# Softplus of a selective scan moved into the matmul's PSUM bank, its bias into ScalarE's operations, with a new order of the side jobs

## The chip, the core and the metric

The kernel runs on one core of a Trainium2 chip. The metric is the device time of one execution in microseconds (us), the median over several runs. A profile of one further execution is at hand. The core has five engines that each work through a queue of their own in order: TensorE (PE in the profile, its weight loads PEld), VectorE (DVE), ScalarE (ACT), GpSimd (POOL) and SyncE (SP, which only issues DMAs here). ScalarE issues DMAs too. Engines wait for one another through semaphores. SBUF is the working memory; PSUM is the memory that TensorE writes its results to, in banks of 512 float32 values for each of the 128 partitions.

## What is computed

The program is a two-layer decoder on 16 blocks of 128 tokens, 512 wide. Five stages follow one another: a state space scan (SSM), a cross attention, a ternary feed-forward network, attention of the second layer, and a mixture of experts. The change lies in the first stage only. In the reference that is:

```python
A = -jnp.exp(A_log)                                   # (512, 16)
dt = jax.nn.softplus(jnp.einsum('bld,ed->ble', x, dt_proj_w) + dt_proj_b)
bc = jnp.einsum('bld,ed->ble', x, x_proj_w) + x_proj_b
Bs, Cs = (bc[..., :d_state], bc[..., d_state:])       # d_state = 16

def step(h, inputs):
    xt, dtt, Bt, Ct = inputs
    dA = jnp.exp(dtt[..., None] * A)
    dBx = (dtt * xt)[..., None] * Bt[:, None, :]
    h = dA * h + dBx
    y = jnp.einsum('bdn,bn->bd', h, Ct)
    return (h, y)
...
return jnp.einsum('bld,md->blm', y, out_proj_w) + out_proj_b
```

Both kernels write softplus(z) as max(z, 0) + ln(1 + exp(-|z|)), with a correction for the rounding of 1 + e: with v = exp(-|z|) and u = 1 + v as rounded, dt = ln(u) + (max(z, 0) - ((u - 1) - v)).

## The kernel before

**Tiling.** The features stand on the partitions (four chunks of 128, `KC`), the tokens on the free axis. Two blocks of tokens make one state (`st` in the code; `BQ` = 2, `TQ` = 256 tokens), so there are eight states. For each state the loop runs over the 16 state dimensions n of the SSM; a pair (state, n) is a unit u, and the loop at lines 371 to 438 goes over all 128 units. I call the position n within a state a step of the loop.

**One unit.** ScalarE makes the decays of unit u+1 (`decays`, line 301: one small copy and four Exp over 254 columns, into the PSUM tile h, two buffers). GpSimd makes dBx of unit u+2 (`terms`, 316; three buffers). VectorE scans unit u (`scan`, 323). For most units VectorE also multiplies by C (tile hC); for the units that `shared` (321) picks, GpSimd does that (tile hs, two buffers). TensorE adds the result into the sums py by transposing (`add`, 338), one unit later, or two for shared ones. B and C of a unit come by a DMA that spreads one row over the partitions (`widths_in`, 311, four units ahead, tile BC, six buffers).

**Side jobs between the units.** At fixed steps n the loop also does, for the next state (`nxt`): `widths` (x_proj) and `widths_out`; the product for the step sizes in two halves h of two chunks each (`step_product`, 194, with the bias as a further small bf16 matmul of a three-row split of dtb against ones); the softplus in `step_exp`, `step_one`, `step_rest`, `step_log`, `step_sum` (204 to 229). The tiles are pd (PSUM), sp_v and sp_u (SBUF), then dt and dtx. For the state behind (`back`): `sums_out`, `turn_back`, `turned_out`, `output` and `output_sum`. And 64 products of keys and values for later stages (`keys_values`, 269), each evacuated by ScalarE (`keys_values_out`, 287) in the following unit and stored by a DMA that ScalarE issues; the last one of a block of tokens also has the next block loaded (`fetch`).

**Order and banks.** In the loop each instruction is pinned to program order on its engine (`pinned`, 71); ahead of the loop the planner of the framework orders them. The side jobs share two PSUM banks, A and B, one buffer each (`bank`, 126). The dictionary `at` (424) says at which steps a key/value product is made and in which bank.

**Ahead of the loop** (lines 130 to 367): the weights are loaded, both bias rows are split into three bf16 rows by GpSimd, then widths, the step sizes of the first state by halves, two loads of ctx, one key/value product, the first decays and the first two dBx.

## Time and profile before

| | us |
|---|---|
| median of three runs (3026.57 to 3032.8) | 3029.26 |
| the profiled execution, its own time | 3033.7 |
| its span, first to last instruction | 3031.8 |
| start of the first scan | 29.66 |
| start of the scan of the last unit | 502.65 |
| mean granted TensorE clock | 0.992 |

Busy time over the whole span: TensorE 2927.2 us (97%), VectorE 1920.5, GpSimd 1490.4, ScalarE 1356.5. The profile gives the line of a helper as L66: it is the line in `Pinned` through which all pinned instructions go, so in the loop instructions are told apart by their tiles. A timeline row reads: start, duration, engine, line, operation, output<-inputs, partitions x elements, count, and in brackets how long the engine had been idle and who released it. The slices of the span are 75.8 us each:

```profile
## 2 busy tenths in 40 slices
PE   8999999999999999999999999999999999999998
PEld 6666665455555555555787556666566666666665
DVE  6989998766776676665887897567643322242224
ACT  5776775333343343345344797655433322222221
POOL 8999996534334334332333663356435553333331
```

### The profile page before, as it was taken

Reading aid. Unit: us, or ns where it says so; the run is one execution under the profiler, and the core shown is the slowest. Engines: PE = TensorE matmul, PEld = TensorE weight load, DVE = VectorE, ACT = ScalarE, POOL = GpSimd, SP = SyncE. Lnnn points to the kernel's source line nnn. Section 1 sums busy time; section 2 is a strip of 40 time slices with the busy share of each in tenths; the row PEclk is TensorE's granted clock in tenths of the full one; section 3 lists DMA queues with packets and bytes.
Section 4 is the critical chain, followed back from the end, with each engine's and each line's share of the span. In section 5 each row is a group of like instructions: output and inputs, shape, how many; then the busy total and the mean of one; then the engine's idle time right before and its main releaser. Section 6 shows DMA issues by size and latency. Waiting matters only on the chain.

```text
span 3031.8 us, 40699 instructions
## 1 busy us (share of the span) xinstructions
PE 2927.2 (97%) x13744; PEld 1830.9 (60%) x13744; DVE 1920.5 (63%) x4221; ACT 1356.5 (45%) x3315; POOL 1490.4 (49%) x1274
## 2 busy tenths in 40 slices
PE   8999999999999999999999999999999999999998
PEld 6666665455555555555787556666566666666665
DVE  6989998766776676665887897567643322242224
ACT  5776775333343343345344797655433322222221
POOL 8999996534334334332333663356435553333331
PEclk9999999999999999999999999999999999999999
DMA  6654444880000000024000200234357665555541
GB/s 199 205 138 126 121 126 135 266 285 14 8 11 11 8 11 11 8 66 143 1 1 1 70 1 8 64 115 164 136 174 241 221 226 164 165 192 165 164 150 61
DMA packets 171603, 331.58 MB, mean 109 GB/s; under 512 B 22078, under 2 KB 80958, under 8 KB 169852
## 3 DMA queue, kind: packets, MB, share of 16 engines
q1 hardware_dynamic: 126988, 219.91, 23.9%
q0 software_dynamic: 19200, 64.16, 6.3%
q10 hardware_dynamic: 25200, 44.84, 3.9%
q8 instruction: 111, 1.82, 0.2%
q14 instruction: 104, 0.85, 0.1%
HBM read 244.57 MB, written 137.43 MB: 126 GB/s over the span
## 4 chain that ended last, share of the span: by engine, by line
PE 67%; DVE 13%; ACT 3%; POOL 1%; issue 1%; DMA 1%; SPq 0%; another core or an unknown queue 0%; DVEq 0%; ACTq 0%; POOLq 0%
PE y L1830 8%; PE pu L1813 7%; PE pg L1813 7%; PE pq L676 7%; PE po L796 6%; PE po L1008 4%; PE ao L785 3%; PE sc L745 3%; PE pt L536 2%; PE pg L988 2%; PE pu L988 2%; PE pT L773 1%; PE ptx L536 1%; PE pkv L66 1%; PE pw L1482 1%
## 5 line engine op out<-in xcount | busy, mean ns | idle before, releaser
L765 POOL TENSOR_TENSOR pr<-pr,sm 128x512 f32<-128x512 f32 x128 | 135.4, 1058 | 369.2 <-DVE sm L764 273.8
L66 POOL TENSOR_TENSOR dBx<-dtx,BC 128x1024 f32<-128x1024 f32 x126 | 298.6, 2394 | 1.0 <-DMA BC<-bcd 0.4
L1813 PE MATMUL pg<-gu,xgT 128*128 128x352 f32 x784 | 297.1, 461 | 1.4 <-ACT act L1816 1.4
L1813 PE MATMUL pu<-gu,xgT 128*128 128x352 f32 x784 | 296.9, 460 | 0.0
L758 ACT ACTIVATE pr<-sc,mx,sf 128x256 f32<-128x256 f32 x256 | 142.2, 560 | 332.8 <-DVE mx L751 304.7
L1817 DVE SCALAR_TENSOR_TENSOR act<-pu,row,act 128x352 f32<-128x352 f32 x98 | 57.1, 582 | 358.4 <-PE pu L1813 339.2
L1830 PE MATMUL y<-dn,aT 128*128 128x512 f32 x588 | 268.3, 592 | 0.0
L1858 POOL TENSOR_TENSOR x<-got,x 128x512 f32<-128x512 f32 x120 | 151.7, 1270 | 225.8 <-DMA got<-results,gidx 224.6
L66 ACT ACTIVATE h<-dt,negA 128x254 f32<-128x254 f32 x508 | 242.2, 477 | 16.9
L796 PE MATMUL po<-w,aT 128*128 128x512 f32 x512 | 233.1, 593 | 1.9 <-DVE aT L790 1.9
L676 PE MATMUL pq<-w,xT 128*128 128x512 f32 x512 | 230.8, 593 | 0.6 <-DVE m L642 0.6
L1851 POOL DMA_INDIRECT got<-results,gidx x120 | 116.2, 969 | 227.6 <-DMA results<-yo 200.5
L66 DVE TENSOR_TENSOR_SCAN h<-h,dBx 128x1024 f32<-128x1024 f32 x80 | 183.2, 2290 | 34.3 <-ACT h L66 24.9
L1813 PEld LDWEIGHTS pu<-gu,xgT 128*128 128x128 f32 x784 | 149.3, 191 | 83.0 <-issue 0.5
L1816 ACT ACTIVATE act<-pg 128x352 f32<-128x352 f32 x98 | 45.5, 464 | 304.5 <-PE pg L1813 265.3
L1813 PEld LDWEIGHTS pg<-gu,xgT 128*128 128x128 f32 x784 | 141.6, 191 | 65.1 <-ACT act L1816 1.9
L647 POOL TENSOR_TENSOR m<-m,m 128x512 f32<-128x512 f32 x96 | 122.5, 1276 | 111.3 <-DVE m L642 108.0
L66 PE MATMUL pkv<-w,cT 128*128 128x512 f32 x384 | 171.6, 593 | 1.4 <-ACT y L66 1.1
L1842 DVE COPY yo<-y 128x512 f32<-128x512 f32 x90 | 62.2, 691 | 165.4 <-PE y L1830 157.9
L1830 PEld LDWEIGHTS y<-dn,aT 128*128 128x128 f32 x588 | 104.1, 190 | 100.8 <-issue 94.2
L1805 ACT COPY xgT<-ptx 128x512 f32<-128x512 f32 x98 | 57.4, 586 | 235.9 <-PE ptx L536 221.4
L998 POOL TENSOR_TENSOR lo<-sg,hi 128x512 fp32r<-128x512 f32 x64 | 84.2, 1316 | 155.4 <-ACT hi L997 155.3
(413 smaller groups left out, 6792.0 us busy)
## 6 DMA issues: line engine op xcount, KB each, us to landing
bucket<-zeros SPq DMA_DIRECT2D x96, 388.0 KB
row<-bucket SPq DMA_DIRECT2D x90, 388.0 KB
BC<-bcd SPq DMA_DIRECT2D x128, 256.0 KB
results<-yo ACTq DMA_DIRECT2D x90, 256.0 KB
gu<-in_moe_guT SPq DMA_DIRECT2D x16, 1408.0 KB
x_k<-kv ACTq DMA_DIRECT2D x32, 256.0 KB
x_v<-kv ACTq DMA_DIRECT2D x32, 256.0 KB
v<-x_v SPq DMA_DIRECT2D x32, 256.0 KB
```

The lines of the kernel that those rows point to most:

```text
L66: return self.tc.keep_in_program_order(call(*args, **kw))
L647: nc.gpsimd.tensor_tensor(m1, m1, m2, ALU.add)
L676: nc.tensor.matmul(ps, src[:, c], w[c], start=c == 0, stop=c == KC - 1)
L758: nc.scalar.activation(pr[:, j], st.sc[g, i][:, j], AF.Exp, scale=st.sf[:, h : h + 1], bias=st.mx[g, i][:, j : j + 1], accum_out=sm[:, j : ...
L765: nc.gpsimd.tensor_tensor(pr, pr, sm.unsqueeze(2).to_broadcast([P, 2, 2 * P]), ALU.mult)
L796: nc.tensor.matmul(st.po, aT[:, j], k.wo[h // 8][:, h % 8], start=h == 0, stop=h == G * J - 1)
L988: nc.tensor.matmul(p[:, e], w[:, c, at : at + P], sn.qT[:, :, c], start=c == 0, stop=c == KC - 1)
L1008: nc.tensor.matmul(sn.po[i], part[:, e, i * P : (i + 1) * P], k.fd[hc // 8][:, hc % 8], start=hc == 0 and part is parts[0], stop=hc == 15 ...
L1813: nc.tensor.matmul(ps, u.xT[:, c], gu[:, c, lo : lo + I], start=c == 0, stop=c == KC - 1)
L1830: self.nc.tensor.matmul(u.y, u.aT[:, c], u.w[1][:, c], start=c == 0, stop=c == 2)
L1851: nc.gpsimd.indirect_dma_start(out=got[:, :], out_offset=None, in_=k.results[h][g][0:end, :], in_offset=bass.IndirectOffsetOnAxis(ap=self. ...
L1858: nc.gpsimd.tensor_tensor(k.x[b], got, k.x[b], ALU.add)
```

## The change

- **Bias.** The step sizes' bias is no longer added by matmuls. It is loaded as a column per chunk (dtb, 128 x 4) and given to ScalarE as the bias of Relu and Abs. Of the two split rows only that of the output projection is left.
- **Softplus in the bank.** Max(z, 0) goes to the SBUF tile sp_m and |z| to sp_u, by ScalarE, chunk by chunk. Exp(-|z|) is written back to pd in PSUM; the correction, the sum and the step size are then computed in pd by VectorE. `step_sum` moves from GpSimd to VectorE; dtx is made by it from pd and x; a new `step_out` has ScalarE copy dt out of the bank.
- **Who multiplies by C.** `shared` now picks seven of 16 units (n = 4, 6, 7, 8, 12, 13, 14) instead of three of eight (1, 4, 6).
- **Positions in a state.** Logs at 6 and 12, rest at 6 and 12, sums at 7 and 13, copies out at 8 and 14; outputs at 5 and 8 and their sums at 6 and 9; the key/value products at new steps and banks.
- **Ahead of the loop.** The order is pinned. The key/value weights and the first ctx loads are issued earlier. The first state's step sizes are computed by quarters (`first_steps`), quarters 0 and 1 in bank A, 2 and 3 in bank B, with max(z + b, 0) made by VectorE. Two key/value products are made in the banks of py.

```diff
-        rows = [cst.tile([65, D], BF16, name=f"rows_{n}") for n in ("dtb", "outb")]
+        dtb = cst.tile([P, KC], F32, name="dtb")
+        row = cst.tile([65, D], BF16, name="row_outb")
...
-        load_row(0)
+        keep(nc.sync.dma_start(dtb, a["dtb"].rearrange("(c p) -> p c", p=P)))
...
-            nc.scalar.dma_start(dtw[:, :, es], a["dtwT"][:, es].rearrange("(c p) e -> p c e", p=P))
...
+            keep(nc.scalar.dma_start(dtw[:, :, es], a["dtwT"][:, es].rearrange("(c p) e -> p c e", p=P)))
+        kvw = k.wslot().rearrange("p (s c e) -> p s c e", s=2, c=KC)
+        for i, n in enumerate(("wk", "wv")):
+            keep(nc.scalar.dma_start(kvw[:, i], a["x2_" + n + "T"].rearrange("(c p) e -> p c e", p=P)))
...
         negA = cst.tile([P, KC, NS], F32, name="negA")
         nc.scalar.activation(negA, alog, AF.Exp)
...
-                    q.nc.tensor.matmul(st.pd[h][:, e], dtw[:, c, at : at + P], st.xT[:, c], start=c == 0, stop=False)
-                q.nc.tensor.matmul(st.pd[h][:, e], rows[0][:, at : at + P], ones, start=False, stop=True)
+                    q.nc.tensor.matmul(st.pd[h][:, e], dtw[:, c, at : at + P], st.xT[:, c], start=c == 0, stop=c == KC - 1)
...
+        def step_exp(st, h):
+            m = wk.tile([P, 2, TQ], F32, tag="sp_m", name="sp_m", bufs=1)
+            u = wk.tile([P, 2, TQ], F32, tag="sp_u", name="sp_u", bufs=1)
+            st.mu[h] = m, u
+            for to, what in ((m, AF.Relu), (u, AF.Abs)):
+                for e in range(2):
+                    q.nc.scalar.activation(to[:, e], st.pd[h][:, e], what, bias=dtb[:, 2 * h + e : 2 * h + e + 1])
+            q.nc.scalar.activation(st.pd[h], u, AF.Exp, scale=-1.0)
 
         def step_one(st, h):
-            v, u = st.vu[h]
-            q.nc.scalar.activation(u, v, AF.Identity, bias=1.0)
+            q.nc.scalar.activation(st.mu[h][1], st.pd[h], AF.Identity, bias=1.0)
+
+        def step_log(st, h):
+            q.nc.scalar.activation(st.dt[:, 2 * h : 2 * h + 2], st.mu[h][1], AF.Ln)
 
         def step_rest(st, h):
-            v, u = st.vu[h]
-            q.nc.vector.scalar_tensor_tensor(v, u, 1.0, v, ALU.subtract, ALU.subtract)
-            q.nc.vector.scalar_tensor_tensor(v, st.pd[h], 0.0, v, ALU.max, ALU.subtract)
+            m, u = st.mu[h]
+            q.nc.vector.scalar_tensor_tensor(st.pd[h], u, 1.0, st.pd[h], ALU.subtract, ALU.subtract)
+            q.nc.vector.tensor_tensor(st.pd[h], m, st.pd[h], ALU.subtract)
 
         def step_sum(st, h):
             hs = slice(2 * h, 2 * h + 2)
-            q.nc.gpsimd.tensor_tensor(st.dt[:, hs], st.dt[:, hs], st.vu[h][0], ALU.add)
-            q.nc.gpsimd.tensor_tensor(st.dtx[:, hs], st.dt[:, hs], st.xT[:, hs], ALU.mult)
+            q.nc.vector.tensor_tensor(st.pd[h], st.dt[:, hs], st.pd[h], ALU.add)
+            q.nc.vector.tensor_tensor(st.dtx[:, hs], st.pd[h], st.xT[:, hs], ALU.mult)
+
+        def step_out(st, h):
+            q.nc.scalar.copy(st.dt[:, 2 * h : 2 * h + 2], st.pd[h])
+
+        def first_steps(st, c, room):
+            h, e = divmod(c, 2)
+            if e == 0:
+                st.pd[h] = bank("AB"[h], [P, 2, TQ], "pd")
+            pd, (m, u) = st.pd[h][:, e], [r[:, c] for r in room]
+            at = c * P
+            for i in range(KC):
+                q.nc.tensor.matmul(pd, dtw[:, i, at : at + P], st.xT[:, i], start=i == 0, stop=i == KC - 1)
+            q.nc.vector.tensor_scalar(m, pd, dtb[:, c : c + 1], 0.0, ALU.add, ALU.max)
+            q.nc.scalar.activation(u, pd, AF.Abs, bias=dtb[:, c : c + 1])
+            q.nc.scalar.activation(pd, u, AF.Exp, scale=-1.0)
+            q.nc.scalar.activation(u, pd, AF.Identity, bias=1.0)
+            q.nc.scalar.activation(st.dt[:, c], u, AF.Ln)
+            q.nc.vector.scalar_tensor_tensor(pd, u, 1.0, pd, ALU.subtract, ALU.subtract)
+            q.nc.vector.tensor_tensor(pd, m, pd, ALU.subtract)
+            q.nc.vector.tensor_tensor(st.dt[:, c], st.dt[:, c], pd, ALU.add)
+            q.nc.gpsimd.tensor_tensor(st.dtx[:, c], st.dt[:, c], st.xT[:, c], ALU.mult)
...
-        shared = lambda u: u % 8 in (1, 4, 6)
+        shared = lambda u: u % 16 in (4, 6, 7, 8, 12, 13, 14)
...
         first = states[0]
+        q.nc = pinned(tc)
+        for _ in range(2):
+            fetch()
         widths(first, xT0)
         widths_out(first)
...
         for u in range(4):
             widths_in(u)
+        room = [wk.tile([P, KC, TQ], F32, tag="hC", name="room", bufs=3) for _ in range(2)]
+        for c in range(KC):
+            first_steps(first, c, room)
         decays(0)
         terms(0)
         terms(1)
+        keys_values(None, ps_y.tile([P, D], F32, tag="py0", name="pkv"))
+        keys_values_out()
+        keys_values(None, ps_y.tile([P, D], F32, tag="py1", name="pkv"))
+        q.nc.scalar.dma_start(outw, a["outwT"].rearrange("(c p) e -> p c e", p=P))
...
             if nxt:
                 if n == 3:
                     widths_out(nxt)
+                if n in (8, 14):
+                    step_out(nxt, n // 14)
                 if n in (5, 9):
                     step_exp(nxt, n // 9)
                 if n in (6, 10):
                     step_one(nxt, n // 10)
+                if n in (6, 12):
+                    step_log(nxt, n // 12)
...
-            if n in (4, 8) and back:
-                output_sum(back, n // 8)
-            if n in (7, 11) and nxt:
-                step_rest(nxt, n // 11)
-            if n in (8, 13) and nxt:
+            if n in (6, 9) and back:
+                output_sum(back, n // 9)
+            if n in (6, 12) and nxt:
+                step_rest(nxt, n // 12)
+            if n in (7, 13) and nxt:
                 step_sum(nxt, n // 13)
...
-                if n in (3, 7):
-                    output(back, n // 7)
+                if n in (5, 8):
+                    output(back, n // 8)
...
-            at = {5: "B", 9: "B", 11: "B", 12: "A", 13: "B", 14: "A", 15: "B"}
+            at = {2: "B", 6: "B", 9: "B", 11: "B", 12: "B", 14: "B", 15: "A"}
             if not back:
-                at |= {0: "A", 1: "B", 3: "B", 7: "B"}
+                at |= {0: "B", 3: "B", 7: "B"}
             if not nxt:
-                at |= {2: "A", 4: "A", 8: "A"}
+                at |= {3: "A", 4: "A", 7: "A"}
...
-            if n in (7, 11) and nxt:
-                step_log(nxt, n // 11)
```

## The prediction

> **What bounds the kernel now.** I read the 40 slices first: the change touches the first stage only, which fills slices 1 to 7, and there TensorE, VectorE and GpSimd all stand at 6 to 9 tenths. Then I cut that stage into the eight states (two blocks of 128 tokens, 16 scan steps each), from each state's second scan to the next's:
>
> ```profile
> core 0: us, PE busy (x) PEld busy (x) DVE busy (x) ACT busy (x) POOL busy (x), PEclk, DMA share, GB/s
> 33.13:94.20 61.07, 59.59 (x364) 47.18 (x365) 54.02 (x31) 43.78 (x100) 55.01 (x27) 0.97 0.73 200
> ...
> 271.71:332.27 60.56, 56.80 (x282) 37.41 (x280) 55.34 (x33) 43.57 (x101) 56.61 (x27) 1.00 0.45 130
> ...
> 453.38:502.65 49.27, 47.94 (x246) 31.51 (x244) 42.37 (x25) 34.80 (x81) 45.61 (x20) 1.00 0.40 122
> ```
>
> A middle state takes 60.56 us (the six of them 359.2 in sum, two being 59.30 and 57.64) while three engines have 55 to 57 us of work. No engine is full, so the time is in waits; VectorE's scan never stops for long, so I read its timeline over one state:
>
> ```profile
> 211.14 2.29 DVE L66 TENSOR_TENSOR_SCAN hs<-h,dBx 128x1024 f32<-128x1024 f32 x1 [1.02 <-POOL dBx L66]
> 215.09 2.30 DVE L66 TENSOR_TENSOR_SCAN h<-h,dBx 128x1024 f32<-128x1024 f32 x1 [1.66 <-ACT h L66]
> ...
> 224.34 0.67 DVE L66 TENSOR_TENSOR x<-po,x 128x512 f32<-128x512 f32 x1
> ...
> 235.24 4.21 DVE L66 SCALAR_TENSOR_TENSOR sp_v<-sp_u,sp_v 128x512 f32<-128x512 f32 x1
> 239.55 0.69 DVE L66 SCALAR_TENSOR_TENSOR sp_v<-pd,sp_v 128x512 f32<-128x512 f32 x1
> 240.16 2.29 DVE L66 TENSOR_TENSOR_SCAN h<-h,dBx 128x1024 f32<-128x1024 f32 x1
> ...
> 253.38 0.83 DVE L66 SCALAR_TENSOR_TENSOR sp_v<-sp_u,sp_v 128x512 f32<-128x512 f32 x1
> 254.32 0.69 DVE L66 SCALAR_TENSOR_TENSOR sp_v<-pd,sp_v 128x512 f32<-128x512 f32 x1
> 254.93 2.28 DVE L66 TENSOR_TENSOR_SCAN hs<-h,dBx 128x1024 f32<-128x1024 f32 x1
> ...
> 267.08 2.30 DVE L66 TENSOR_TENSOR_SCAN h<-h,dBx 128x1024 f32<-128x1024 f32 x1 [0.42 <-POOL dBx L66]
> ```
>
> The same operation, both inputs in SBUF, takes 0.83 us once and 4.21 once. GpSimd's timeline says why:
>
> ```profile
> 234.23 4.66 POOL L66 TENSOR_TENSOR dBx<-dtx,BC 128x1024 f32<-128x1024 f32 x2
> 240.38 1.26 POOL L66 TENSOR_TENSOR dt<-dt,sp_v 128x512 f32<-128x512 f32 x1 [1.49 <-DVE sp_v L66]
> ```
>
> VectorE's operation ends 0.56 us after GpSimd's two products (238.89) and GpSimd then waits for it. The operations with one input in PSUM (0.69, and 0.67 at 224.34 in the middle of GpSimd's work) are not stretched. Also GpSimd reaches the end of a state late: VectorE waits 0.42 and 1.02 us for dBx.
>
> **Part 1, softplus in the bank (middle state).** Removed from VectorE: the two halves of step_rest, 235.24 to 240.16 and 253.38 to 254.93, so 4.92 + 1.55 = 6.47 us. Added: step_rest and step_sum, four operations per half, each with one operand in PSUM and one in SBUF, the form of the 0.69 row. The second of each pair needs the first: 0.72 (spacing of the dependent L519 operations, 0.70 each) + 0.65, so 1.37 a pair, four pairs: 5.5. The result in PSUM has a row too (the scan, 2.30 in PSUM, 2.29 in SBUF).
>
> **Part 2, who multiplies by C.** Seven of 16 steps instead of six are shared with GpSimd. VectorE loses one product (scan plus product 3.5 us from start to start, scan alone 2.3): -1.2. GpSimd gains 2.33 and loses step_sum (4 x 1.27 = 5.1): 57.0 of work becomes 53.5 to 54.3. So its lag at the state's end goes: -0.42 - 1.02 = -1.4. The shared steps now come in runs (6, 7, 8 and 12, 13, 14); in the first run GpSimd has 3 x 4.65 = 14.0 us against 10.5 on VectorE, a lag of 3.5, but terms are issued two steps ahead (about 6 us), so it is covered.
>
> Sum for a middle state: 60.56 - 6.47 + 5.5 - 1.2 - 1.4 = 57.0, with the waits for ScalarE (1.66 and 1.09) kept. From the state of 57.64 the same steps (4.13 removed) give 56.1. I take 56.9 for each.
>
> **Can the others follow?** TensorE for a state: 16 adds at 0.875, seven key/value products at 3.44, two outputs at 3.66, step sizes 2 x 3.43, widths 1.75, turns 0.9: 54.9 (before, with four bias products of 0.13: 55.4). ScalarE: 16 decays at 2.14, seven evacuations with their DMA issue at 0.98, and 4.2 for bc, sums_out and turned_out, so 45.2; per half the four Relu and Abs with a bias column, then Exp, one, Ln and the copy step_out. The nearest row for the four is bc, the same column bias out of PSUM at 256 wide:
>
> ```profile
> L66 ACT ACTIVATE bc<-pb,xpb 32x256 f32<-32x256 f32 x7 | 3.1, 448 | 0.0
> ```
>
> 4 x 0.45 + 0.63 + 0.63 + 0.63 + 0.58 = 4.3 a half, 8.6 against 4.9 before: ScalarE has 53.8. Bounds: 0.37 apiece (difference of 512 and 256 rows) to 0.51 (spacing of the 254-wide decays): 8.0 to 9.1. All four fit below 56.9, with little room. I laid the slots of a state out in order for the four engines with these durations. Tightest is step 8: add, output and step product, 8 us of TensorE; step_exp of step 9 then waits for the product until 35.3 us into the state, and the decays behind it in ScalarE's queue release scan 11 about 0.4 us late. The rest closes at 56.7.
>
> [...]
>
> **Part 3, ahead of the loop.** Before, the first scan starts at 29.66. The new first_steps work by quarters, two to a bank. Does one engine wait for another at a different column of one bank? A later stage shows it:
>
> ```profile
> 1638.09 0.62 ACT L1204 ACTIVATE sv<-pkv,al 128x128 f32<-128x128 f32 x2 [0.81 <-PE pkv L1200]
> ...
> 1638.74 0.29 DVE L1209 TENSOR_TENSOR kr<-pkv,l_cos 128x128 f32<-128x128 f32 x1 [2.11 <-ACT sv L1204]
> ```
>
> VectorE needs nothing that ScalarE makes there, only other columns of pkv, and starts when ScalarE ends, after 2.11 us. So I take it that quarter 1's matmuls wait for quarter 0's whole chain (behind them on TensorE stand quarters 2 and 3 and two key/value jobs): m 0.42, Abs 0.45, Exp 0.48, one 0.45, three on VectorE at 0.42 (256-wide row, L510), 7 handovers of 0.05: 3.4 us. The first quarter's product ends at 14.05 as now; 17.4; product 1.7; 22.5; quarter 2's product is hidden but its m queues behind quarter 1 on VectorE; 25.9; product of quarter 3 in the same bank 1.7, or 3.2 if TensorE is slow after idling (after 5.08 us idle at 33 us, eight adds took 1.97 instead of 1.04); 31.0 to 32.5; dtx 0.65; dBx 2.35; scan 0 at 34.0 to 35.5: **+5** (4.3 to 6). If banks don't serialize: ScalarE's 1.75 a quarter sets the pace, scan 0 at 24.9: **-4.7**. That is the low bound.
>
> [...]
>
> Moved, at no cost: the two key/value weights (0.97 us of ScalarE's issue) go ahead of negA, into ScalarE's idle time up to 8.60, and their 2 MB ahead of bc's write. That write landed at 18.6; some 6 us later at worst (2 MB at the 350 GB/s that the DMA view shows there), plus BC's 0.4 + 5.6, is 30.6, under the 31.7 of the first dBx; uncovered it would cost the difference. The ctx loads go ahead of BC on SP (0.94 us of issue, same cover). GpSimd's dtb preparation (4.8 us, over at 12.64) was hidden. A third key/value job is done before scan 1, which makes up for TensorE's later start.
>
> **First and last state.** State 0 loses 5.95 of step_rest, gains 5.5, -1.2, -1.4, and its ScalarE waits (0.57, 0.68, 0.58, 2.43) shrink by about 1 with one job fewer: 57 (-4; bounds 0 to -5). The last state is TensorE's: ten jobs in both, but eight instead of seven stand ahead of the last decays: +3.44, less idle now filled: **+2.2** (0 to 3.4).
>
> **Sum.** 6 x 56.9 - 359.2 = -17.8; state 0 -4; last +2.2; start +5: **-14.6**. Behind the last scan VectorE's chain of norm and sines sets the end as before (502.65 to 520.3), so all of it arrives: span 3031.8 to 3017. That execution took 3033.7, 4.4 over the median of 3029.26; off the median: **3015**.
>
> **Rivals.**
> 1. Banks don't serialize: start -4.7, so 3005. For it: nothing but that the quarters were put so; against it the 2.11 us. 17%.
> 2. ScalarE's queue takes part of it. In the list of waits (total us, times, longest)
>
> ```profile
> ACT kv L66 <- PE pkv L66: 20.0, 23, 2.0
> ```
>
> evacuations wait for TensorE 23 times, with decays queued behind them. If states come to 58.7: -7, -2.4, +2.2, +5: 3027. 15%.
> 3. Slower: TensorE slips one job per state at step 8. One wait of 0.6 us or more for its bank B there (output_sum 6, key/value job, evacuation, output follow each other within 8 us) delays step_exp 9, and with it decays 11 and scan 11, one for one; a whole job, 3.44, makes states of 60.3: +2.8, -0.7, +2.2, +5 = +9, 3038. Against it: the laid-out slots keep 0.4 us there. 10%.
> 4. The change doesn't do what it says, VectorE is still stretched beside GpSimd (3.4 in seven states): 3038. The 14 undisturbed 0.67 rows speak against it. 3%.
>
> **Numbers.** The forecast, 55%, spans 3008 to 3022 (states of 56 to 58, start 4 to 6). Range 3003 to 3028: takes in rival 1 and most of 2. About 0.2%, 6 us, is what can be told from no change: faster 0.72, same 0.15, slower 0.13.
>
> **What would show it.** Right: states of 56 to 58 us; no VectorE operation on pd over 0.75; no wait for dBx at steps 0 and 1; TensorE idle 3 us twice before 30 us; first scan at 34 to 36; last state longer than 49.3. Wrong: first scan at 25 (step 3); scan 11 waiting for decays by over 1 us in every state (slot sum); ScalarE's Relu over 0.51.

## The result and the profile after

The changed kernel is slower. Its median is 3034.93 us (3030.86 to 3037.3, 14 runs) against 3029.19 us (3023.52 to 3032.8, 14 runs) for the kernel before in the same series: ratio 1.0018, 95% interval 1.0011 to 1.0026, so 5.7 us more where 14 less were forecast. A second series gave 1.0032 (1.0023 to 1.0041).

The profiled execution took 3033.84 us with a span of 3032.1, almost that of before (3031.8). The totals agree by chance: the execution profiled before the change lies 4.5 us over its median, the changed one 1.1 under its own. In these two profiles the first stage ends later (first projection of the next stage at 538.7 instead of 532.1 us, +6.6), and a stretch of a later stage, the output products pw from first to last, took 267.5 us instead of 274.0. Over the profiles of this study that stretch took 264 to 275 us, whatever was edited in the first stage. So I use a profile for the first stage, and the timed ratio for the whole.

The first stage, cut at the starts of scans as before (from each state's second scan to the next state's; the last stretch ends at the scan of the last unit):

| | before | changed | difference | forecast |
|---|---|---|---|---|
| first scan | 29.66 | 36.44 | +6.8 | +5 |
| state 0 | 61.07 | 63.54 | +2.5 | -4 |
| state 1 | 58.70 | 61.67 | +3.0 | -1.8 |
| states 2 to 6, sum | 300.48 | 288.95 | -11.5 | -16.0 |
| last stretch | 49.27 | 56.18 | +6.9 | +2.2 |
| last scan at | 502.65 | 510.25 | +7.6 | -14.6 |

A second profiled execution of the changed kernel (after_again below) gave 61.91, 62.65, 288.92 and 54.49 us for the states and the last stretch, and the last scan at 508.44: the loss at the edges is there again, but state 0 and the last stretch are 1.6 and 1.7 us shorter.

(The forecast's 56.9 for each of states 1 to 6 is split here: 56.9 - 58.70 and 5 x 56.9 - 300.5. The first and second scan of state 0 are 3.47 us apart in both.) Busy times of the changed kernel in four of these stretches; columns as in the windows of before:

```profile
core 0: us, PE busy (x) PEld busy (x) DVE busy (x) ACT busy (x) POOL busy (x), PEclk, DMA share, GB/s
39.91:103.45 63.54, 57.94 (x345) 44.90 (x344) 51.92 (x35) 46.33 (x108) 52.91 (x24) 0.97 0.69 187
103.45:165.12 61.67, 58.17 (x253) 35.91 (x251) 53.11 (x37) 46.66 (x109) 54.46 (x24) 0.97 0.71 204
...
222.68:280.36 57.68, 56.40 (x300) 39.48 (x299) 53.09 (x36) 46.43 (x109) 53.51 (x24) 1.00 0.50 130
454.07:510.25 56.18, 52.82 (x251) 33.31 (x250) 41.19 (x25) 35.21 (x82) 45.92 (x20) 0.97 0.49 114
```

A middle state comes near what was worked out: 57.68 us against 56.9, VectorE 53.1 and GpSimd 53.5 busy. States 0 and 1 have hardly more work and are 6 and 4 us longer. TensorE was idle for 5.60, 3.50 and 3.36 us in states 0, 1 and the last one, and for 1.28 in the middle one. Its mean granted clock is 0.97 in those three and 1.00 in the middle one; it was 0.69 and 0.68 over the slow matmuls after two of these waits (last section) and 0.56 over the x_proj of state 1 (109.00 to 112.16 us).

VectorE's timeline over state 2:

```profile
179.47 2.30 DVE L66 TENSOR_TENSOR_SCAN h<-h,dBx 128x1024 f32<-128x1024 f32 x1 [1.57 <-ACT h L66]
...
186.30 0.70 DVE L66 SCALAR_TENSOR_TENSOR pd<-sp_u,pd 128x512 f32<-128x512 f32 x1 [0.43 <-ACT sp_u L66]
187.03 0.69 DVE L66 TENSOR_TENSOR pd<-sp_m,pd 128x512 f32<-128x512 f32 x1
...
189.84 0.67 DVE L66 TENSOR_TENSOR pd<-dt,pd 128x512 f32<-128x512 f32 x1
190.54 0.69 DVE L66 TENSOR_TENSOR dtx<-pd,xT 128x512 f32<-128x512 f32 x1
...
202.13 2.30 DVE L66 TENSOR_TENSOR_SCAN h<-h,dBx 128x1024 f32<-128x1024 f32 x1 [1.19 <-ACT h L66]
...
213.42 2.29 DVE L66 TENSOR_TENSOR_SCAN hs<-h,dBx 128x1024 f32<-128x1024 f32 x1 [0.50 <-PE py L66]
```

The operation that took 4.21 us takes 0.70, and all 56 operations of the softplus on VectorE in the seven states lie between 0.67 and 0.70. The waits for decays add up to what they were, 2.76 us after 2.75, but they stand elsewhere: before at steps 2 and 7 (1.66 in the forecast's rows, and the row below), now at steps 5 and 11 (1.57 and 1.19). Two more waits are new, 0.43 for sp_u and 0.50 for an hs tile.

```profile
231.76 2.30 DVE L66 TENSOR_TENSOR_SCAN h<-h,dBx 128x1024 f32<-128x1024 f32 x1 [1.09 <-ACT h L66]
```

The same view at the places where states 0, 1 and the last one lose:

```profile
63.83 0.70 DVE L66 SCALAR_TENSOR_TENSOR pd<-sp_u,pd 128x512 f32<-128x512 f32 x1 [3.62 <-ACT sp_u L66]
...
74.01 2.29 DVE L66 TENSOR_TENSOR_SCAN hs<-h,dBx 128x1024 f32<-128x1024 f32 x1 [5.25 <-PE py L66]
...
121.08 2.30 DVE L66 TENSOR_TENSOR_SCAN h<-h,dBx 128x1024 f32<-128x1024 f32 x1 [4.85 <-ACT h L66]
...
484.58 2.29 DVE L66 TENSOR_TENSOR_SCAN hs<-h,dBx 128x1024 f32<-128x1024 f32 x1 [6.33 <-PE py L66]
...
507.94 2.29 DVE L66 TENSOR_TENSOR_SCAN hs<-h,dBx 128x1024 f32<-128x1024 f32 x1 [3.79 <-PE py L66]
```

Three kinds of wait: for the softplus at step 6, for the decays at step 5 of state 1, and for TensorE to free an hs tile (releaser py: the add that reads the tile). The last kind is new. hs has two tiles, and with three shared units in a row (6, 7, 8) the scan of step 8 needs the tile of step 6. TensorE's timeline says why it is late in state 0:

```profile
60.51 3.60 PE L66 MATMUL pkv<-w,cT 128*128 128x512 f32 x8
67.13 5.46 PE L66 MATMUL pkv<-cT,w 128*128 128x128 f32 x32 [3.02 <-ACT kv L66]
72.43 1.04 PE L66 MATMUL py<-ident,hs 128*128 128x128 f32 x8
```

The key/value products of steps 6 and 7 both use bank B. The second waits 3.02 us for the evacuation of the first, then runs slowly (5.46 us; 3.84 after the same wait in the second execution), and the add of step 6 stands behind it.

### The profile page after: what moved, and what is told of

The parts are those of the page before. It is cut to its first block, busy times and chain, and to the rows that moved or that the text cites. A ratio compares the mean times of both kernels' runs of the same rounds, so it can differ in the third digit from the quotient of the medians.

```text
span 3032.1 us, 40667 instructions
## 1 busy us (share of the span) xinstructions
PE 2927.1 (97%) x13712; PEld 1831.3 (60%) x13712; DVE 1906.4 (63%) x4253; ACT 1380.2 (46%) x3379; POOL 1463.6 (48%) x1247
## 4 chain that ended last, share of the span: by engine, by line
PE 67%; DVE 11%; ACT 2%; issue 1%; DMA 1%; POOL 1%; SPq 0%; DVEq 0%; ACTq 0%; POOLq 0%
PE y L1843 8%; PE pg L1826 8%; PE pu L1826 8%; PE pq L689 7%; PE po L809 6%; PE po L1021 4%; PE ao L798 3%; PE sc L758 3%; PE pt L549 2%; PE pg L1001 2%; PE pu L1001 2%; PE pw L1495 2%; PE pT L786 1%; PE ptx L549 1%; PE ps L1410 1%
## 5 line engine op out<-in xcount | busy, mean ns | idle before, releaser
L66 DVE TENSOR_TENSOR_SCAN h<-h,dBx 128x1024 f32<-128x1024 f32 x72 | 164.8, 2289 | 26.7 <-ACT h L66 23.1
L1818 ACT COPY xgT<-ptx 128x512 f32<-128x512 f32 x98 | 57.5, 587 | 234.4 <-PE ptx L549 224.7
```

The costliest lines, as they stand in the source:

```text
L66: return self.tc.keep_in_program_order(call(*args, **kw))
```

## The experiments

All are edits of the changed kernel; e11_all and e12_more_start combine several. The ratio is to the kernel before in the same series, with its 95% interval; the changed kernel itself gave 1.0018 and 1.0032 in two series, so a difference of that size between two rows says nothing. "Start" counts from the first max(z, 0) on VectorE to the first scan, because that point itself lies at 13.4 to 16.2 us from execution to execution (last section).

| kernel | ratio | first scan (start) | state 0 | state 1 | states 2-6, mean | last | last scan |
|---|---|---|---|---|---|---|---|
| changed | 1.0018 [1.0011, 1.0026] | 36.44 (22.98) | 63.54 | 61.67 | 57.79 | 56.18 | 510.25 |
| e1_four_banks | 1.0002 [0.9993, 1.0011] | 31.81 (16.13) | 61.82 | 61.68 | 57.79 | 54.51 | 502.47 |
| e2_first_state | 1.0018 [1.0009, 1.0026] | 39.04 (23.35) | 62.63 | 61.91 | 57.79 | 56.21 | 512.21 |
| e3_last_state | 1.0048 [1.0034, 1.0063] | 36.88 | 63.58 | 61.50 | 57.81 | 56.03 | 510.53 |
| e7_five_shared | 1.0014 [1.0005, 1.0023] | 38.93 (23.19) | 63.31 | 62.04 | 57.95 | 52.46 | 509.99 |
| e5_old_shared | one run | 36.50 | 61.63 | 62.09 | 58.95 | 52.52 | 510.94 |
| e6_sbuf_exp | one run | 39.09 | 63.70 | 61.50 | 58.35 | 56.18 | 515.68 |
| e8_late_pieces | 1.0016 [1.0006, 1.0026] | 39.06 | 63.55 | 57.65 | 57.76 | 56.18 | 508.69 |
| e9_first_last | 1.0031 [1.0019, 1.0042] | 38.78 | 63.24 | 61.68 | 57.78 | 53.71 | 509.77 |
| e10_start | 1.0010 [1.0001, 1.0019] | 31.01 (14.86) | 63.41 | 62.39 | 57.80 | 56.18 | 507.24 |
| e11_all | 0.9982 [0.9972, 0.9992] | 28.71 (14.22) | 58.14 | 57.92 | 57.97 | 50.43 | 491.99 |
| e12_more_start | 0.9960 [0.9947, 0.9974] | 25.54 (11.72) | 60.64 | 58.15 | 57.95 | 50.42 | 487.98 |
| after_again | 1.0032 [1.0023, 1.0041] | 36.99 | 61.91 | 62.65 | 57.78 | 54.49 | 508.44 |

after_again is the changed kernel once more. Its states show how much a stretch varies by itself: the middle ones by 0.01 us, states 0 and 1 and the last one by 1 to 1.7. Smaller differences in those three columns say nothing (the 61.82 and 54.51 of e1_four_banks, for one). In state 0 and the last stretch the 1.6 and 1.7 us are one thing: after the same waits of TensorE the same matmuls took 5.46 and 5.40 us in one execution, 3.84 and 3.70 in the other (last section).

**The start: do banks serialize?** The quarters were put in four banks instead of two, nothing else.

```diff
-            if e == 0:
-                st.pd[h] = bank("AB"[h], [P, 2, TQ], "pd")
-            pd, (m, u) = st.pd[h][:, e], [r[:, c] for r in room]
+            pool, tag = ((ps_p, "A"), (ps_p, "B"), (ps_y, "py0"), (ps_y, "py1"))[c]
+            pd, (m, u) = pool.tile([P, TQ], F32, tag=tag, name="pd"), [r[:, c] for r in room]
```

> The four quarters of first_steps each get a bank of their own (A, B and the two of py); the order of the instructions stays. Theory (two engines do not share a bank, so the matmuls of quarters 1 and 3 wait for the chain ahead of them): the matmuls run through without a stop, only VectorE's order is left, 3.2 us a quarter from 13.5, so the first scan starts at 29 to 30.5 instead of 36.4, and the time falls by 5 to 7 us. Rival (it is the pinned order on VectorE alone, the bank costs nothing): the first scan stays at 35 to 37 and the time within 2 us.

TensorE in the changed kernel up to the first scan, and then in this one:

```profile
11.42 1.99 PE L66 MATMUL pd<-xT,w 128*128 128x256 f32 x8 [0.56 <-ACT bc L66]
16.79 5.41 PE L66 MATMUL pd<-xT,w 128*128 128x256 f32 x16 [3.37 <-DVE dt L66]
26.74 3.11 PE L66 MATMUL pd<-xT,w 128*128 128x256 f32 x8 [4.55 <-DVE dt L66]
```

```profile
11.86 9.60 PE L66 MATMUL pd<-xT,w 128*128 128x256 f32 x32 [0.56 <-ACT bc L66]
```

With two banks TensorE waits twice (3.37 and 4.55 us), for VectorE's last operation (dt) of the quarter before in the same bank, though it needs none of its data. With four banks all 32 matmuls run through in 9.60 us. The start shrinks from 22.98 to 16.13 us, by 6.9. What is left is VectorE's order: a quarter's max(z, 0) stands behind the whole tail of the quarter before, 3.19 us from one to the next (15.68, 18.88, 22.07, 25.26). The whole falls to that of the kernel before, the lowest ratio of the single edits; of the 7.8 us at the last scan 3.4 are the shorter state 0 and last stretch that after_again has, too. That it is the bank that makes TensorE wait isn't shown by this alone: each quarter also got a tile of its own here, and a shared tile seems to be enough: in e11_all below, two products go to the two halves of one tile h (1024 columns, 512 to each product, so by size two banks), and the second starts when ScalarE has copied the first (25.96 + 0.58), after 3.40 us:

```profile
25.96 0.58 ACT L66 COPY kv<-h 128x512 f32<-128x512 f32 x1
```

```profile
26.59 5.19 PE L66 MATMUL h<-w,cT 128*128 128x512 f32 x8 [3.40 <-ACT kv L66]
```

Two tiles in one bank no run tried.

**State 0: the extra products moved.** First to steps 0, 1 and 5:

```diff
-                at |= {0: "B", 3: "B", 7: "B"}
+                at |= {0: "B", 1: "A", 5: "B"}
```

> The three extra key/value products of the first state are made at steps 0, 1 and 5 (banks B, A, B) instead of 0, 3 and 7 (all B). Theory (products of neighbouring steps in one bank make TensorE wait for ScalarE, the adds stand behind them, and the scan of step 8 waits for a tile that add 6 has to free): the waits of 3.6 and 5.3 us on VectorE in the first state go, it takes 55 to 58 us instead of 63.5, and the second state, whose loads were bunched up by that stall, 58 to 60 instead of 61.7; time -6 to -10 us. Rival (the first state is slow because TensorE has just idled and runs at a lower clock, or because of the loads of weights): first state over 61.

State 0 took 62.63: VectorE's waits of 3.62 and 5.25 became five of 0.62 to 4.07. A miss.

Then to 0, 5 and 8, the slots of the outputs that state 0 doesn't have, with the last state's extras moved in the same kernel:

```diff
-                at |= {0: "B", 3: "B", 7: "B"}
+                at |= {0: "B", 5: "B", 8: "B"}
...
-                at |= {3: "A", 4: "A", 7: "A"}
+                at |= {4: "A", 8: "A", 13: "A"}
```

> The changed kernel, with the three extra key/value products of the first state at steps 0, 5 and 8 (bank B, where the other states have their outputs) instead of 0, 3 and 7, and those of the last state at 4, 8 and 13 (bank A, where the other states have their step sizes' products) instead of 3, 4 and 7. Theory: in the first state the product at step 3 makes the step sizes' product of step 4 late, and VectorE waits 3.62 us for the softplus at step 6; the pair 6 and 7 in one bank makes the add of unit 6 late, and VectorE waits 5.25 us for its hs tile. Both go: state 0 takes 57.5 to 59.5 instead of 63.5. In the last state the wait of 6.33 at step 8 goes, but the one at step 14 can grow as it did with products at 4, 10 and 13: the last stretch takes 51 to 56 instead of 56.2. Rival: TensorE has a fixed amount of work in both states and is the bound there; the waits come back at other steps: state 0 stays above 62 and the last stretch at 56.

State 0 missed again (63.24), by another loop through three engines. TensorE in that kernel, then VectorE:

```profile
70.95 5.19 PE L66 MATMUL pd<-xT,w 128*128 128x256 f32 x16 [2.92 <-ACT dt L66]
75.98 3.73 PE L66 MATMUL pkv<-cT,w 128*128 128x128 f32 x32
```

```profile
85.16 2.30 DVE L66 TENSOR_TENSOR_SCAN h<-h,dBx 128x1024 f32<-128x1024 f32 x1 [6.69 <-ACT h L66]
```

The second step product waits for ScalarE to copy dt out of bank A (2.92), then takes 5.19 us (3.62 to 3.72 in states 0 and 2 of the changed kernel), the key/value product of step 8 follows, ScalarE waits 5.95 us for it (by its timeline) with the decays of scan 11 queued behind. As long as ten products stand in the loop of state 0, they came back as waits in all three placements (61.6 to 63.7 over all kernels). With three products ahead of the loop and only nine in it state 0 took 58.14 (e11_all) and 60.64 (e12_more_start). Both share their kernel with other edits, so the share of the one product isn't shown by itself, and what would have held state 0 at 57 stays open.

**The last state.** Its extras were moved to 4, 10 and 13, so that seven products instead of eight stand ahead of the last decays:

```diff
-                at |= {3: "A", 4: "A", 7: "A"}
+                at |= {4: "A", 10: "A", 13: "A"}
```

> The three extra key/value products of the last state are made at steps 4, 10 and 13 (bank A) instead of 3, 4 and 7. Theory (at steps 6 and 7 two products stand ahead of add 6, for which scan 8 waits, and scan 8 in turn holds output_sum, for which the product of step 9 waits): the wait of 6.3 us at scan 8 goes, the stretch from the last state's second scan to the last scan takes 48 to 51 us instead of 56.2, time -5 to -8 us. Rival (the last state is bound by the sum of TensorE's work, wherever the products stand): 54 or more.

56.03 instead of 56.18: the wait at step 8 fell from 6.33 to 3.03, and that at step 14 grew from 3.79 to 7.65, again for an hs tile. (The ratio of 1.0048 is above the changed kernel's although the profile's first stage ends at 539.2, 0.5 later than there; I can't explain it.) So the count of products alone wasn't it. Placed at 4, 8 and 13 (e9_first_last) the stretch took 53.71, 0.8 below the second execution of the changed kernel, which says nothing either; its waits for hs tiles are 3.03 and 7.23. In e7_five_shared hs and hC share one ring of five tiles instead of two and three:

```diff
-                hC = wk.tile([P, KC, TQ], F32, tag="hs", name="hs")
+                hC = wk.tile([P, KC, TQ], F32, tag="hC", name="hs", bufs=5)
...
-                hC = wk.tile([P, KC, TQ], F32, tag="hC", name="hC", bufs=3)
+                hC = wk.tile([P, KC, TQ], F32, tag="hC", name="hC", bufs=5)
```

> The two tiles hs and the three tiles hC become one ring of five, so that a scan whose product GpSimd makes needs the tile of five steps ago and no longer that of the shared step before the last; the space is the same and nothing else changes. Theory: all waits of the scan for TensorE's add (5.3 us in the first state, 6.3 and 3.8 in the last, 0.5 in each middle state) go; first state 58 to 61 us, middle states 57.0 to 57.5 instead of 57.8, last state 49 to 53; time -8 to -14 us. Rival (these waits only stand in for TensorE being late, so that the decays behind ScalarE's evacuations come late by as much): all within 3 us of the changed kernel.

VectorE's waits between 30 and 515 us (total us, times, longest), the two largest of the changed kernel, then the largest of this one:

```profile
DVE h L66 <- ACT h L66: 23.1, 14, 4.8
DVE hs L66 <- PE py L66: 19.4, 11, 6.3
```

```profile
DVE h L66 <- ACT h L66: 37.7, 24, 5.3
```

The 19.4 us of waits for TensorE are gone, and 14.6 us more of waits for decays stand in their place. In the last state there is a gain (52.46, against 56.18 and 54.49 in the two executions of the changed kernel); in state 0 all is given back, because ScalarE's evacuations wait for the same late products. The middle states, expected at 57.0 to 57.5, took 57.95: the wait of 0.50 at step 14 went, and one of 0.63 for decays stands at step 15. Together with the placement 4, 8, 13 (e11_all and e12_more_start) the last stretch takes 50.4.

**State 1: transfers or the product at step 2?** The eight loads of the query weights were moved from units 14 to 21 to units 22 to 29.

```diff
-            if u >= 6:
+            if u >= 6 and not 14 <= u < 22:
                 next(pieces, None)
```

> The changed kernel, with the eight loads of the query weights (4 MB in all, issued in units 14 to 21) moved to units 22 to 29. The question is why state 1 takes 61.7 us where the later states take 57.7. Theory: between 100 and 120 us the transfers are full (DMA share 1.0, some 300 to 340 GB/s), so that xT of the next state lands 10.5 us after its issue and ScalarE's own issues wait for a free lane; x_proj comes late, the evacuation behind it too, and the decays behind that in ScalarE's queue. With the loads later, state 1 takes 57.6 to 58.5 and the whole 3 to 4 us less. Rival: it is the key/value product at step 2, whose evacuation stands ahead of decays in ScalarE's queue, with what state 0 left behind on TensorE: state 1 stays at 61 to 62 and the total within 1 us of the changed kernel's.

State 1 took 57.65 us, 4.0 less, and the states after it what they took in the changed kernel. The chain in the changed kernel, TensorE and then ScalarE:

```profile
109.00 3.23 PE L66 MATMUL pb<-xT,xpw 128*32 128x256 f32 x8 [0.86 <-DMA xT<-in_xT]
112.16 4.00 PE L66 MATMUL pkv<-w,cT 128*128 128x512 f32 x8
```

```profile
116.19 0.59 ACT L66 COPY kv<-pkv 128x512 f32<-128x512 f32 x1 [3.44 <-PE pkv L66]
...
118.79 0.17 ACT L66 COPY h<-zero 128x8 f32<-128x8 f32 x1 [1.14 <-DMA w<-in_xa_wqT]
```

xT of the next state was issued at 98.40 and landed 10.5 us later, x_proj came late (and took 3.23 us at a mean granted clock of 0.56; 1.91 in state 2), the product of step 2 behind it too, and its evacuation stands ahead of decays; then ScalarE waits 1.14 us more before its next work, by the profile for a load of the weights, which SyncE had issued; what ties its work to that load no row shows. From 100 to 110 us the DMA share was 1.05 at 336 GB/s. Before the change the same loads ran at 0.92 and 302 GB/s (90 to 100 us), xT was issued 11.6 us ahead of its use, and no product stood at steps 0 to 4 of a middle state. So it is the transfers, and not what state 0 left behind, which still took 63.55. That the new product at step 2 is what lets them reach the scan fits the rows, but no run moved that product alone. In the total the gain doesn't show (1.0016): this profile's first scan was 2.6 us later, and the interval is 6 us wide.

**Middle states: what are the parts worth?** The old choice of shared units:

```diff
-        shared = lambda u: u % 16 in (4, 6, 7, 8, 12, 13, 14)
+        shared = lambda u: u % 8 in (1, 4, 6)
```

> The changed kernel with one thing undone: GpSimd multiplies by C in three units of eight again (n = 1, 4, 6, 9, 12, 14), not in seven of sixteen. The question is what the seventh shared unit is worth in a middle state (57.6 to 58.3 us in the changed kernel). Theory A, the prediction's: VectorE's chain sets the pace, and one more multiplication there costs 3.5 - 2.3 = 1.2 us: middle states of 58.6 to 59.2 (GpSimd has lost the step sum and isn't late any more, so no wait for dBx comes back). Rival: ScalarE's decays set the pace of a middle state, VectorE's 1.2 us go into its waits for them (1.57 at step 5 and 1.20 at step 11): middle states stay at 57.5 to 58.0. In the last state the scans no longer wait for TensorE to hand back an hs tile at steps 8 and 14 (6.33 and 3.79 in the changed kernel), because the shared units no longer come in threes; both theories say so.

Middle states of 58.89 to 59.03, above the changed kernel's by 1.20 to 1.35 in four of five (0.70 in the fifth): theory A. No wait for dBx came back. The last stretch is 52.52 without runs of three shared units (54.49 and 56.18 with them). This and the next kernel ran once each; the middle states of the changed kernel agree to 0.03 us between its two executions. And Exp kept in SBUF, max(z, 0) in the bank:

```diff
-            for to, what in ((m, AF.Relu), (u, AF.Abs)):
+            for to, what in ((u, AF.Abs), (st.pd[h], AF.Relu)):
...
-            q.nc.scalar.activation(st.pd[h], u, AF.Exp, scale=-1.0)
+            q.nc.scalar.activation(m, u, AF.Exp, scale=-1.0)
...
-            q.nc.vector.scalar_tensor_tensor(st.pd[h], u, 1.0, st.pd[h], ALU.subtract, ALU.subtract)
-            q.nc.vector.tensor_tensor(st.pd[h], m, st.pd[h], ALU.subtract)
+            q.nc.vector.scalar_tensor_tensor(m, u, 1.0, m, ALU.subtract, ALU.subtract)
+            q.nc.vector.tensor_tensor(st.pd[h], st.pd[h], m, ALU.subtract)
```

> The changed kernel, with Exp(-|z|) kept in an SBUF tile and max(z, 0) written back into the bank instead: the same instructions, but VectorE's first operation of the correction reads two SBUF tiles, as before the change. Theory: an operation with two SBUF inputs is stretched while GpSimd works, whatever else was changed: this operation takes 0.83 us alone and up to 4.2 beside GpSimd's dBx, and middle states grow from 57.7 to between 58.5 and 61.5. Rival: the stretch belonged to the old places of the work (rest at steps 7 and 11), and here the operation takes 0.7 to 0.85 both times: middle states stay within 57.6 to 58.2.

VectorE's two such operations in state 3 of that kernel, then GpSimd beside them:

```profile
247.24 1.88 DVE L66 SCALAR_TENSOR_TENSOR sp_m<-sp_u,sp_m 128x512 f32<-128x512 f32 x1 [0.59 <-ACT sp_u L66]
...
269.54 0.67 DVE L66 SCALAR_TENSOR_TENSOR sp_m<-sp_u,sp_m 128x512 f32<-128x512 f32 x1
```

```profile
246.21 2.36 POOL L66 TENSOR_TENSOR hs<-hs,BC 128x1024 f32<-128x1024 f32 x1 [0.38 <-DVE hs L66]
248.53 2.80 POOL L66 TENSOR_TENSOR dBx<-dtx,BC 128x1024 f32<-128x1024 f32 x1
...
269.70 2.72 POOL L66 TENSOR_TENSOR hs<-hs,BC 128x1024 f32<-128x1024 f32 x1 [1.30 <-DVE hs L66]
```

The first starts while GpSimd is at work, and ends (249.12) 0.55 us after GpSimd's operation does (248.57), as the 4.21 before the change ended 0.56 behind GpSimd's pair. The second starts 0.16 us ahead of GpSimd, takes 0.67, and it is GpSimd's operation that is longer (2.72 instead of 2.36). So in these two meetings the one that came second took longer. Middle states grew by 0.56 on average, to 58.15 to 58.87, between the two expectations: the theory's cause, near the rival's size, because only one of two operations met GpSimd, and it waited for one GpSimd operation where the 4.21 waited for two.

**A version that beats both.** The new start alone first: all four products and maxima ahead of the chains, in four banks.

```diff
+            pool, tag = ((ps_p, "A"), (ps_p, "B"), (ps_y, "py0"), (ps_y, "py1"))[c]
...
+        for c in range(KC):
+            first_product(first, c, room)
         for c in range(KC):
             first_steps(first, c, room)
```

> The changed kernel with a new start only: the four quarters of the first step sizes in four different banks (A, B and the two of py), and all four products with their max(z, 0) issued ahead of the quarters' chains, so that neither a bank nor VectorE's order makes one quarter wait for another. Theory: counted from the first max(z, 0) on VectorE, which starts at 13.5 or, where the matmuls before it run at the lower rate, at 15.7 us, there follow 0.5 for it, 4 x 1.75 of ScalarE's four operations, 1.4 of VectorE, 0.73 for dtx and 2.4 for dBx, 12.0 in all: the first scan starts at 25.5 or 27.7 us. That is 10.5 to 11 earlier than in the changed kernel from the same point (23.0 there), and, with states 0 and 1 unchanged at 61.5 to 63.5 and 61.7, the whole comes to a ratio of 0.9975 to 0.999. Rival: banks are not the cause, VectorE's order is only half of it, and something else (ScalarE waiting for VectorE at each quarter, or the spread of B and C, landing near 23) holds the first dBx: first scan at 28 or later from a start at 13.5, total no better than with four banks alone (1.0002).

The start took 14.86 us, not 12.0: VectorE's tails had to wait for the fourth maximum in its order (first tail at 22.34, though ScalarE had finished the first quarter at 18.4), and the second scan waited 1.68 us for decays behind an evacuation. The ratio of 1.0010 is no better than that of four banks alone, as the rival had it. Then all together:

```diff
+        spare = ps_h.tile([P, KC, BQ, P], F32, tag="h", name="h")
...
+        for i in range(2):
+            keys_values(None, spare[:, 2 * i : 2 * i + 2].rearrange("p c b t -> p (c b t)"))
+            keys_values_out()
+        keys_values("A")
...
-                at |= {0: "B", 3: "B", 7: "B"}
+                at |= {0: "B", 5: "B"}
...
-                at |= {3: "A", 4: "A", 7: "A"}
+                at |= {4: "A", 8: "A", 13: "A"}
```

(with e7's ring and e8's later loads)

> All that the runs so far point to, together: the new start of the run before, with three key/value products instead of two ahead of the loop (two of them in a spare tile of h, so that TensorE has work while the chains run), extras of the first state at steps 0 and 5 only, the query weights' loads eight units later, one ring of five tiles for hs and hC, and the last state's extras at steps 4, 8 and 13. Theory: first scan at 25.5 to 28, state 0 at 58 to 60, states 1 to 6 at 57.6 to 58.0, last stretch at 50 to 53; the last scan starts at 486 to 491 instead of 502.7 before the change, and the whole takes 11 to 16 us less than before: ratio 0.9945 to 0.9965. Rival: TensorE's work in the stage is fixed, and what starts earlier waits for it in the last state: the last stretch grows to 58 or more and the ratio stays at 0.998 or above.

The ratio is 0.9982 (0.9972 to 0.9992). The last scan came at 491.99, 1 us after the expected range, and the whole gained about half of what was expected: 5.4 us. That is the rival's ratio without its reason: the last stretch took 50.4 us, not 58. And with the start mended:

```diff
+            for c in range(KC + 1):
+                if c < KC:
...
+                if c:
...
+        keys_values(None, spare[:, 0:2].rearrange("p c b t -> p (c b t)"))
         decays(0)
+        keys_values_out()
...
+        keys_values("A")
+        decays(1)
+        keys_values_out()
+        keys_values("B")
...
-            if u + 1 < len(units):
+            if 0 < u < len(units) - 1:
                 decays(u + 1)
...
-                at |= {0: "B", 3: "B", 7: "B"}
+                at |= {0: "A", 5: "B"}
```

(with the rest of e11_all; the product of step 0 goes to bank A, because B now holds the third product made ahead of the loop)

> The combined kernel with a mended start. In it VectorE held the tails of the quarters behind the fourth product (first tail at 20.07 though ScalarE had finished the first quarter at 16.77), and the second scan started at 35.65 instead of some 32.2, because an evacuation that waited 5.28 us for TensorE stood ahead of the decays of unit 1. Now the tail of a quarter follows the next quarter's max(z, 0), the first key/value product goes to the spare tile of h and the other two to banks A and B, and the decays of unit 1 stand ahead of the second evacuation. Theory: the first scan starts 12.1 us after the first max(z, 0), at 25.6 to 27.8 us (28.71 in the combined kernel), the second 3.5 behind it at 29 to 31.5 (35.65), and the last scan 4 to 6.5 us earlier than the combined kernel's 491.99: ratio 0.996 to 0.998. Rival: the widths of B and C, for which GpSimd waited 4.85, 1.25 and 1.22 us at 40 to 48 us there, set the pace of the first units, and TensorE the rest: the second scan comes earlier, the fifth doesn't, and the ratio stays at 0.9975 or above.

Ratio 0.9960 (0.9947 to 0.9974), 11.8 us less than before at the medians (3014.54 against 3026.34). TensorE at the start of that kernel, and its windows:

```profile
11.76 7.20 PE L66 MATMUL pd<-xT,w 128*128 128x256 f32 x32 [0.55 <-ACT bc L66]
18.80 3.73 PE L66 MATMUL h<-cT,w 128*128 128x128 f32 x32
22.37 3.60 PE L66 MATMUL pkv<-w,cT 128*128 128x512 f32 x8
25.80 3.73 PE L66 MATMUL pkv<-cT,w 128*128 128x128 f32 x32
```

```profile
29.02:89.66 60.64, 57.14 (x341) 44.11 (x339) 51.93 (x35) 46.60 (x108) 53.13 (x24) 0.97 0.69 207
...
437.56:487.98 50.42, 47.32 (x237) 30.69 (x236) 41.19 (x24) 34.56 (x81) 46.97 (x21) 1.00 0.46 117
```

TensorE goes through the start without a pause, and the last stretch holds 47.3 us of its work in 50.4. The second scan started 6.6 us earlier than in e11_all and the fifth 6.3, against the rival; state 0 gave 2.5 of it back and the last scan came 4.0 earlier. Of the 2.5, 1.7 are slow matmuls after one wait of 2.92 us (5.41 us here, 3.72 in e11_all; mean granted clock over state 0 0.97 and 1.00).

Last, the changed kernel again:

> The changed kernel itself, once more, on the same chip as the mended start, to have its stages from a second execution. Expected: ratio 1.001 to 1.003; first scan at 36.4 to 36.9 or at 38.8 to 39.1 (the two values that kernels with its start have shown), states 63.5, 61.5 to 62, then 57.6 to 58.3, last stretch 56.2. If the first scan takes either value for the same kernel, the 2.5 us between them belong to the execution and not to an edit.

It took the lower of the two start values a second time (36.99), so the question wasn't settled with one kernel; that all kernels with its start share the same work up to there is what speaks for the execution.

## Why the prediction was wrong, point by point

**Part 1, softplus in the bank: right.** Four operations a half were forecast at 2.74 us together and took 2.74 (0.68, 0.70, 0.67, 0.69 by their medians). The contention with GpSimd as the cause of the 4.21 holds (e6_sbuf_exp: 1.88 us behind GpSimd's operation, 0.67 ahead of it), but a part of its size was the old place: at the new one it would cost 1.2 and 0.56 of it would arrive.

**Part 2, who multiplies by C: right.** -1.2 forecast, 1.20 to 1.35 measured in four states of five (e5_old_shared). The waits for dBx at steps 0 and 1 went as said. What wasn't seen is the price of three shared units in a row with two hs tiles. The text counted only GpSimd's lag over them and called it covered; that TensorE's add must free the tile of step 6 before the scan of step 8 isn't in it.

**Can the others follow: right in kind, 0.9 short.** TensorE has 56.4 us of work in a state instead of 54.9 (the count was short before the change, too: 55.4 against 56.80 in the windows), ScalarE's Relu and Abs took 0.47 and 0.48 instead of 0.45. The decays were to release scan 11 about 0.4 us late; it was 1.19 to 1.33 in the middle states. The waits of before at steps 2 and 7, which the sum kept, went, and so it came near by luck. States 2 to 6 took 57.8 instead of 56.9. The two new waits, 0.43 and 0.50, add up to that, but e7_five_shared removed the second and gained nothing, so what the 0.9 us hang on isn't shown. Of the 16.0 us forecast there, 11.5 came. (By the starts of the second scans the states given as 59.30 and 57.64 took 58.70 and 58.24; from 58.24 the same steps give 57.0, not 56.1, and the 56.9 hardly moves.)

**Part 3, the start: right mechanism, a size off.** TensorE idles twice, 36.44 instead of 34.0 to 35.5. The product of quarter 1 was taken at 1.7 us and took 3.4 after the wait of 3.37 (16.79 to the next max(z, 0) at 20.22); the working allowed for slow matmuls at quarter 3 only. That TensorE waits for another engine at other columns of a shared bank and tile was my estimate from one wait of VectorE's of 2.11 us; it is now shown by TensorE's own two, 3.37 and 4.55 us, which e1_four_banks doesn't have. Which of the two counts, bank or tile, is not shown.

**First and last state: this step failed.** "State 0 [...] 57 (-4; bounds 0 to -5)" subtracted the middle state's gain, and "The last state [...] +2.2 (0 to 3.4)" priced the one product more. I had laid the slots of a middle state out for four engines and let the other two follow by sums, though their products stand at other steps. The runs put in their place: in state 0 the products of steps 3 and 7 make TensorE late for the softplus of step 6 and the hs tile of step 8 (+2.5 instead of -4, +0.8 in the second execution). TensorE's work there fell from 59.59 to 57.94 us (56.48), but its idle time rose from 1.48 to 5.60 (5.43); other placements moved the waits and didn't remove them. In the last state the one product is 3.44, and VectorE (for hs) and TensorE (for po, which VectorE adds to x) wait for each other, which adds 2.0 of idle time; the other 1.4 go with slow matmuls:

```profile
476.54 7.03 PE L66 MATMUL pkv<-w,cT 128*128 128x512 f32 x16
...
490.97 5.40 PE L66 MATMUL pkv<-w,cT 128*128 128x512 f32 x8 [2.00 <-DVE x L66]
```

The 16 matmuls are the products of steps 6 and 7, the add stands behind them; the eight below took 5.40 us instead of 3.60 after an idle time of 2.00. TensorE was busy for 52.82 us in this stretch and for 47.94 before, and idle for 3.36 and 1.33: 4.9 + 2.0 = 6.9. In the second execution the eight took 3.70 and the stretch 54.49, 5.2 more than before: +2.2 was too low without the slow matmuls, too.

**State 1: a second omission.** It was counted as a middle state (56.9) and took 61.67. That its transfers were full before, too, stood in the windows of before: a DMA share of 0.73 in state 0 and 0.65 in state 1 (a row that the forecast left out), 0.45 later. The forecast checked moved loads ahead of the loop only, not those that the loop itself issues, against the new product at step 2.

**The rivals.** The first (no serialization) is refuted by TensorE's two waits and by e1_four_banks, which removed them. The second (ScalarE's queue) has its waits, 1.57 and 1.19, but those of before went in exchange; states came to 57.8, not 58.7. The third had the right mechanism, TensorE one job late through bank B, and put it at step 8 of every state instead of in the first and last. The fourth is refuted by the 0.67 to 0.70. The signs listed as right came true, for the states from 2 on, to half a microsecond. One listed as wrong came true as well, scan 11 waiting for decays by over 1 us in each of states 1 to 6, and it said little, since waits of that size had stood elsewhere before. The total was still wrong: the list named only what the working had laid out.

Against 14.6 forecast at the last scan, +7.6 came: 22.2 us, of which state 0 is 6.5, state 1 4.8, the last state 4.7, states 2 to 6 4.4 and the start 1.8. In the second execution +5.8 came. At the median 5.7 us more were measured.

## What to carry to other kernels

Lay out the slots of the first and the last pass of a pipelined loop as carefully as those of the steady one: here the steady states gained 11.5 us and the edges lost 19 (17 in the second execution). When a side job moves, ask of every ring it shares (PSUM banks, small rings of SBUF tiles, an engine's queue with work for the main chain behind) which release it now stands in front of. Put independent chains that start a stage into banks and tiles of their own (6.9 us of the start here, e1_four_banks), and order the engine that serves them so that one chain's tail follows the next one's head (e12_more_start, which has this order, took 11.72 us for the start, e11_all 14.22).

## What the runs showed of the hardware

**TensorE's rate at the start has two values.** The eight matmuls of the first quarter took 1.99 us in the changed kernel and 3.78 in e2_first_state, with the same instructions ahead of them. Windows from 11.4 to 15.5 us in the two kernels (PE busy first, the granted clock third from the end):

```profile
11.40:15.50 4.10, 1.99 (x8) 1.44 (x8) 0.67 (x2) 1.43 (x4) 2.77 (x4) 1.00 1.02 366
```

```profile
11.40:15.50 4.10, 3.64 (x8) 2.52 (x8) 0.00 (x0) 0.41 (x1) 2.79 (x4) 1.00 1.01 364
```

The granted clock is 1.00 in both, so the record of the throttle doesn't show this halving (it does show the slow matmuls below). It moved the first scan by about 2.5 us between profiles. X_proj ahead of these matmuls was busy for 3.2 to 3.6 us; 3.59 us stand ahead of the high rate in after_again and of the low one in e2_first_state, so what decides isn't shown.

**The same short wait of TensorE costs in one execution and not in the next.** After 3.02 us idle 32 matmuls took 5.46 us in the first profile of the changed kernel, and after 2.00 us eight took 5.40 (rows above). In the second profile, after the same waits:

```profile
67.68 3.84 PE L66 MATMUL pkv<-cT,w 128*128 128x128 f32 x32 [3.02 <-ACT kv L66]
...
490.86 3.70 PE L66 MATMUL pkv<-w,cT 128*128 128x512 f32 x8 [2.00 <-DVE x L66]
```

While these matmuls ran, the mean granted clock was 0.69 and 0.68 in the first profile, and 1.00 while the product ahead of the first wait ran (3.60 us). The differences, 1.6 and 1.7 us, are those of state 0 (63.54 and 61.91) and of the last stretch (56.18 and 54.49). Both values come again in the edited kernels; what decides between them no run shows.
